# Order of the head's first operations, and rows of A gathered by GpSimd for half of the last level, in a graph layer on one core

## The chip, the cores and the metric

The kernel runs on one core of a Trainium2 chip. The metric is the device time of one execution in microseconds (us). The engines are called as the profile calls them: PE (TensorE; PEld is its loading of weights), DVE (VectorE), ACT (ScalarE), POOL (GpSimd) and SP (SyncE, which here only issues DMAs).

## The reference, cut to what matters

One layer of a graph network over 12500 nodes with 64 features and 212500 edges, sorted by their destination. `row` is the source of an edge, `col` its destination; sums go to the source.

```python
h = jnp.maximum(_layernorm(x, axis=-1), 0.0)
edge_in = jnp.concatenate([h[row], h[col], dist], axis=1)      # 64 + 64 + 1
e = jax.nn.silu(edge_in @ eW1 + eb1)                           # 128
e = jax.nn.silu(e @ eW2 + eb2)
agg = jax.ops.segment_sum(e, row, num_segments=h.shape[0])
node_in = jnp.concatenate([h, agg], axis=1)
out = x + jax.nn.silu(node_in @ nW1 + nb1) @ nW2 + nb2
```

## The kernel before

The first product splits into A = h @ eW1[:64] for the source, B = h @ eW1[64:128] for the destination, and a term of the edge weight. Nodes are dealt to 100 buckets of 125 (node = l * 100 + b). The tables `ta` (A) and `tb` (B) lie in DRAM with 256 floats for each node: a part rounded to fp32r and the remainder, each of 128.

**Sending.** Edges go in 208 blocks of 1024. For each block a window of `tb` is loaded (`load`), PE picks the rows (`qp`, line 531), ACT copies them to `qs` with the place l + 1 of the source in its bucket behind them (lines 543, 546), and POOL scatters 128 rows at a time to DRAM `q` by indirect DMAs (line 553), to places that VectorE has counted (`count`, lines 457 to 485). `q` then holds, bucket by bucket, the row Q of every edge without its A.

**Steps.** 14 levels take so many ranks of every bucket; a level goes over 25 batches of 4 buckets, a batch has n steps (1 or 2) of 512 edges, 450 steps in all. In the first and in the last level n is 1. `fetch` loads a batch's Q (`qt`, SP), `fetch_a` its A rows (`a`, SP, 512 KB, a ring of 3 buffers). A step is cut in pieces that `turn` puts in a fixed order (PE, DVE, ACT and SP run in the order written; POOL's queue is made by the framework):

- `s_one`: DVE compares the places with 1 to 125, which gives the one-hot `one` (line 719), three steps ahead.
- `s_turn`, `s_one_t`: PE turns it (`lr`, line 668), ACT copies it (`oneT`, line 673), two steps ahead.
- `s_pt`: PE transposes Q into `pt` (line 685) and adds A by products of A's two parts with `oneT` (line 692); ACT takes silu (line 701). One step ahead. It also asks for the next Q and A (`fetch` up to 4 batches ahead, `fetch_a` 3), and in the last level for the node's inputs (`nodes_in`: `xr`, to which POOL adds the bias at line 335, and `zo`).
- `s_bias`, `s_p2`: the second product and silu (lines 730, 736, 740).
- `s_seg`, `s_add`: PE sums by source (line 753), DVE adds to `aggT` (lines 762, 764).
- In the last level `nodes` follows each batch: PE's z product into the bank `misc` (line 348), ACT's silu (349), PE's o product (358), DVE's `os` (361) and its copy of the next `zo` into `misc` (363), and the store.

Four hooks in a step (`None` in `turn`) take in pieces of the sending, of `made_a`, of the feed (the `tb` rows) and of the node's tail.

**Level 0.** `made_a` makes A itself for each batch: it loads hT (`hrl`, line 642), multiplies (288), splits (292, 295), writes `ta` (647), computes the node part `zos` (651, 654) into a buffer of which there is one, and writes it to `own` (656).

**Head.** The first rows of x are normed (`norm`), multiplied (`first_rows`) and written to a small table, the first destinations (`destinations`) and sources (`sources`) are turned into places; the order of these operations is written out by hand, and so are the queues.

Of the kernel before, what the change touches and what calls it, by code (L numbers as in the profile page):

```python
# [28 lines left out]
F32 = mybir.dt.float32  # L29
# [3 lines left out]
I32 = mybir.dt.int32  # L33
# [6 lines left out]
P = 128  # L40
# [39 lines left out]
def tile_gnn(ctx: ExitStack, tc: tile.TileContext, x, src, dst, ew, eW1, eb1, eW2, eb2, nW1, nb1, nW2, nb2, out):  # L80
# [108 lines left out]
    def load_sources(h):  # L189

        at = h * BLK
        for p0, p1, n in ((0, 96, BLK), (96, NP - 1, BLK), (NP - 1, NP, min(BLK, LAST - at))):
            nc.sync.dma_start(srcR[p0:p1, at : at + n], vec(src, p0 * PAIR + at, p1 - p0, n))
# [81 lines left out]

    tb0 = dram.tile([P * NE, 2 * H], F32, name="tb0")
    tb00 = dram.tile([P * G, 2 * H], F32, name="tb00")
    ta_buckets, tb_buckets = (t.rearrange("(l b) f -> l b f", b=NB) for t in (ta, tb))

    def product(s, hr, ps, tag, to):  # L280
# [93 lines left out]
    with work:  # L374
# [21 lines left out]
        def load_rows(s):  # L396

            if s < nblocks and (s < 4 or stored):
                p, g = s // 2, s % 2
                if g == 0:  # L400
                    for a in range(2):
                        at = a * HB + WL
                        nc.sync.dma_start(extras[p % 2][at : at + 2], ews[:, p, :, a])
# [9 lines left out]
        def load(s):  # L413

            if s < nblocks:
                p, g = s // 2, s % 2
                win = wins[p % NW]
                table, end = (tb0, NE * P) if s < EARLY else (tb, NB * P)
                if s < 2 * FIRST_PAIRS:
                    table, end = tb00, G * P  # L420
                assert s < EARLY or len(done_b) == NB // G
                if g == 0:
                    of = identb[:, p % HB :: HB][:, :, None].to_broadcast([P, 2, HB])
                    nc.scalar.copy(sels[p % NW].rearrange("p (a m) -> p a m", a=2), of)
                    at = nc.sync.value_load(base_i[:, p : p + 1], min_val=0, max_val=end - SPAN)
                    for a in range(2):
                        rows = table[bass.ds(at, SPAN), :]
                        of = [[2 * H, WL], [4 * STEP * H, 2], [1, 2 * H]]
                        of = bass.AP(tensor=rows.tensor, offset=rows.offset + 2 * a * STEP * H, ap=of)
                        nc.sync.dma_start(win[a * HB : a * HB + WL, :, a].rearrange("p g k h -> p g (k h)"), of)  # L430
                blk[s] = [win[:, g], ld.tile([P, HALF], F32, name="pick")]
            load_rows(s + 1)
# [172 lines left out]
        def fetch(i):  # L605
            if i >= len(batches):
                return
            c, B, n = batches[i]
            assert not any(pending[: c + 1])
            at = B * G * ROWS + G * (ENDS[c] - n * P)  # L610
            qt = ld2.tile([P, G * most, W], F32, name="qt")
            ins = nc.sync.dma_start(
                qt[:, : G * n, :].rearrange("p j w -> p (j w)"),
                q[at : at + G * n * P, :].rearrange("(p j) w -> p (j w)", p=P),
            ).ins
            for later in range(c + 1, len(LEVELS)):
                tc.declare_no_dep(ins, group=f"rows{later}", reason="these ranks were full before")
            tc.add_manual_dep(ins, last_rows[LEVELS[c][1] - 1].name, AFTER)
            tc.add_to_no_dep_group("loads", ins)
            batch[c, B] = [qt, None, None]  # L620

        def fetch_a(i):

            if i >= len(batches):
                return
            c, B, n = batches[i]
            a = lda.tile([P, G, 2 * H], F32, name="a")
            if c == 0:
                making[B] = made_a(B, a)
                next(making[B])  # L630
            else:
                nc.sync.dma_start(a, ta_buckets[:, B * G : B * G + G])
            batch[c, B][1] = a
# [3 lines left out]
        def made_a(B, a):  # L637

            while B not in done_b:
                next(feed)  # L640
            hr = late.tile([P, G // 2, P], F32, name="hrl")
            nc.sync.dma_start(hr, hd[:, B * G // 2 : (B + 1) * G // 2, :])
            for _ in range(3):
                yield
            yield from product(0, hr, mm, "mm", a.rearrange("p g (k h) -> p g k h", k=2))
            yield
            nc.sync.dma_start(ta_buckets[:, B * G : B * G + G], a)
            zo = [mm.tile([P, G // 2, L], F32, name="zo", tag="mm") for _ in range(2)]
            for h in range(2):
                half = slice(h * D, (h + 1) * D)  # L650
                nc.tensor.matmul(zo[h], w1n[half, :], hr[half, :, :L], start=True, stop=True)
            zos = late1.tile([P, G * L], F32, name="zos")
            for h in range(2):
                nc.scalar.copy(zos.rearrange("p (i a l) -> p i a l", a=2, l=L)[:, :, h], zo[h])
            yield
            nc.sync.dma_start(own[:, B, :], zos)
            yield

        def of(k):
# [2 lines left out]
            return batch[c, B], [((g * G + t) % n * G + (g * G + t) // n, (g * G + t) // n) for t in range(G)]  # L662

        def s_turn(k):
            tops = st[k]["one"].rearrange("p g l -> p (g l)").bitcast(BF16)
            lr = mm.tile([L, G, P], F32, name="lr", tag="mm")
            for t in range(G):
                nc.tensor.matmul(lr[:, t, :], tops[:, 2 * t * L + 1 : 2 * (t + 1) * L : 2], identb, start=True, stop=True)  # L668
            st[k]["lr"] = lr

        def s_one_t(k):
            oneT = wk.tile([L, G, P], F32, name="oneT")
            nc.scalar.copy(halves(oneT), st[k].pop("lr"))  # L673
            st[k]["oneT"] = oneT

        def s_pt(k):

            (qt, a, _), tiles = of(k)
            c, B, _, _ = steps[k]
            for _ in making.pop(B, ()) if c == 0 else ():  # L680
                pass
            oneT = st[k].pop("oneT")
            pt = mm.tile([P, G, P], F32, name="pt", tag="mm")
            for t, (j, _) in enumerate(tiles):
                nc.tensor.matmul(  # L685
                    pt[:, t, :], qt[:, j, :H], ident, is_transpose=True, start=t == 0, stop=False, skip_group_check=True
                )
            for b, same in itertools.groupby(range(G), lambda t: tiles[t][1]):
                same = list(same)
                cols = slice(same[0], same[-1] + 1)  # L690
                for i in range(2):
                    nc.tensor.matmul(  # L692
                        pt[:, cols, :],
                        halves(a[:L, b, i * H : (i + 1) * H]),
                        halves(oneT[:, cols, :]),
                        start=False,
                        stop=i == 1,
                        skip_group_check=True,
                    )
            e1 = wk.tile([P, G, P], F32, name="e1")  # L700
            nc.scalar.activation(e1, pt, AF.Silu)  # L701
            st[k]["e1"] = e1
            c, B, n, g = steps[k]
            if c == len(LEVELS) - 1:
                node_in[B] = nodes_in(B, ndp[0])
            if g == n - 1:
                i = c * (NB // G) + B
                while len(fetched) <= i + NQ and (len(fetched) < final or i + 3 >= final):
                    fetched.append(0)
                    fetch(len(fetched) - 1)  # L710
                fetch_a(c * (NB // G) + B + NA)
# [247 lines left out]
        with listing:  # L959
# [5 lines left out]
            consts, zone_ = tables(), zones()  # L965
            next(rows_)
            next(consts)
            next(lists_)
            limits()
            next(rows_)  # L970
            next(firstw)
            next(lists_)
            nc.scalar.copy(halves(three2[:, 0, :]), three)
            nc.gpsimd.tensor_tensor(three2[:, 1, :], three, three2[:, 0, :], op=OP.subtract)
            last_rows_of(wins[0])
# [2 lines left out]
                last_rows_of(win)  # L978
            for xs in xss:
                nc.gpsimd.memset(xs, 0.0)  # L980
            next(rows_)
            next(src0)
            next(lists_)
            next(made[0])
            for part_ in (src0, made[0], firstw, made[0], made[0], lists_, src0, consts):
                next(part_)
            load_rows(0)
            load(0)
            load_sources(1)
            load(1)  # L990
            for part_ in (lists_, zone_):
                next(part_)
# [29 lines left out]
        aggT = aggp.tile([P, NB, L], F32, name="aggT")  # L1022
        late = work.enter_context(tc.tile_pool(name="late", bufs=3))
        late1 = work.enter_context(tc.tile_pool(name="late1", bufs=1))
        ld2 = work.enter_context(tc.tile_pool(name="ld2", bufs=NQ))
        lda = work.enter_context(tc.tile_pool(name="lda", bufs=NA))
        ones_ = work.enter_context(tc.tile_pool(name="ones", bufs=NO))
# [202 lines left out]
```

## Time and profile before

| | us |
|---|---|
| median of 3 runs | 3503.77 |
| lowest and highest | 3501.37, 3517.39 |
| the profiled execution's own time | 3483.84 |
| its span in the profile | 3482.0 |

In the views, a row of the timeline has start, duration, engine, line, operation, out<-in and the idle time of the engine ahead of it with what ended it. L719 is line 719; "q" behind an engine's name is its sequencer, which issues DMAs. A row of groups has the count, busy time and mean of one in ns. Times are of one profiled execution. "issue" is time in which an engine waited for nothing that the profile shows.

### The profile page before, as it was taken

How to read it: one execution, taken by the hardware profiler on the slowest of the kernel's cores; microseconds unless marked ns; L12 is line 12 of the kernel's file. 1: busy time of each engine (PE TensorE's matmuls, PEld its weight loads, DVE VectorE, ACT ScalarE, POOL GpSimd, SP SyncE). 2: the span in 40 equal slices, each digit the busy share in tenths (PEclk: the TensorE clock that was granted, in tenths of full speed). 3: DMA queues.
4: the chain of work that ended last, by engine and by line, in shares of the span. 5: the costliest groups of instructions: out<-in, count | busy, mean ns of one | idle time of the engine just before them, and what ended most of it. 6: DMA issues, size and time to landing. Idle time of an engine off the chain costs nothing. (4 is left out here: it accounts for less than half of the span.)

```text
span 3482.0 us, 47653 instructions
## 1 busy us (share of the span) xinstructions
PE 2344.1 (67%) x16730; PEld 2160.0 (62%) x16772; DVE 1842.7 (53%) x2884; ACT 1380.4 (40%) x3001; POOL 1641.7 (47%) x1724
## 2 busy tenths in 40 slices
PE   4445777735776567656765676767777767776799
PEld 3234666634665567556755666766676766766797
DVE  8775566554546445544454444455554554555443
ACT  3223444322444344334433444434443434443454
POOL 7665555465445544444445444444444544444401
PEclk7555778866887788778877888888888888888899
DMA  4344566654544345445553445455555655555586
GB/s 153 136 162 165 174 203 213 196 165 144 175 147 155 130 137 169 137 133 157 170 169 130 146 163 161 145 160 165 171 169 152 186 163 163 172 175 158 164 260 188
DMA packets 243744, 572.56 MB, mean 164 GB/s; under 512 B 47069, under 2 KB 106133, under 8 KB 243191
## 3 DMA queue, kind: packets, MB, share of 16 engines
q1 hardware_dynamic: 160308, 393.28, 36.6%
q0 software_dynamic: 53408, 122.68, 9.8%
q10 hardware_dynamic: 29782, 53.47, 4.8%
q8 instruction: 136, 2.23, 0.3%
q14 instruction: 110, 0.90, 0.1%
HBM read 349.93 MB, written 219.27 MB: 163 GB/s over the span
## 5 line engine op out<-in xcount | busy, mean ns | idle before, releaser
L553 POOL DMA_INDIRECT q<-qs,to x1661 | 1604.8, 966 | 1672.4 <-ACT qs L546 1174.1
L692 PE MATMUL pt<-oneT,a 125*128 125x128 f32 (+1 forms) x2800 | 491.9, 320 | 621.3 <-ACT oneT L673 518.8
L692 PEld LDWEIGHTS pt<-oneT,a 125*128 125x128 f32 x2800 | 415.3, 222 | 667.8 <-ACT oneT L673 552.5
L701 ACT ACTIVATE e<-pt 128x512 f32<-128x512 f32 x450 | 268.9, 598 | 1087.3 <-PE pt L692 374.4
L764 DVE TENSOR_TENSOR aggT<-aggT,seg 128x500 f32<-128x500 f32 x324 | 218.3, 674 | 876.0 <-remote 266.0
L736 PE MATMUL p<-w,e 128*128 128x128 f32 x3600 | 597.1, 319 | 0.0
L753 PE MATMUL seg<-one,e 128*128 128x125 f32 x3592 | 557.8, 303 | 51.1 <-DVE aggT L764 32.8
L736 PEld LDWEIGHTS p<-w,e 128*128 128x128 f32 x3600 | 548.1, 230 | 24.3 <-issue 22.4
L753 PEld LDWEIGHTS seg<-one,e 128*128 128x128 f32 x3592 | 498.1, 213 | 69.7 <-DVE aggT L764 37.9
L531 PE MATMUL qp<-win,pick 128*128 128x256 f32 x1664 | 379.4, 363 | 101.0 <-issue 49.2
L719 DVE TENSOR_TENSOR one<-misc,qt 128x500 f32<-128x500 f32 x425 | 286.0, 673 | 288.7 <-remote 75.4
L531 PEld LDWEIGHTS qp<-win,pick 128*128 128x128 f32 x1664 | 299.6, 248 | 184.1 <-issue 85.0
L543 ACT COPY qs<-qp 128x512 f32<-128x512 f32 x418 | 245.5, 588 | 406.4 <-issue 147.2
L740 ACT ACTIVATE e<-p 128x512 f32<-128x512 f32 x450 | 268.9, 598 | 278.8 <-remote 151.4
L465 DVE TENSOR_REDUCE each<-oh 128x100 bf16<-128x800 bf16 x208 | 318.3, 1530 | 7.2
L673 ACT CAST oneT<-lr 125x512 fp32r<-125x512 f32 x450 | 263.8, 586 | 101.8 <-remote 49.2
L685 PE MATMUL pt<-ident,qt 128*128 128x128 f32 x1800 | 284.8, 282 | 11.4 <-issue 5.0
L481 DVE TENSOR_TENSOR terms<-oh,misc 128x800 f32<-128x800 bf16 x208 | 203.6, 979 | 128.2 <-remote 95.4
L730 ACT COPY p<-b2f 128x512 f32<-128x512 f32 x450 | 267.1, 593 | 0.0
L685 PEld LDWEIGHTS pt<-ident,qt 128*128 128x128 f32 x1800 | 220.6, 147 | 28.5 <-issue 12.9
L483 DVE TENSOR_REDUCE rank<-terms 128x8 f32<-128x864 f32 x208 | 219.0, 1053 | 7.2
L668 PEld LDWEIGHTS <-one 128*125 128x125 bf16 x1800 | 197.5, 161 | 28.4 <-issue 27.0
(163 smaller groups left out, 1736.7 us busy)
## 6 DMA issues: line engine op xcount, KB each, us to landing
a<-ta SPq DMA_DIRECT2D x325, 512.0 KB
qt<-q SPq DMA_DIRECT2D x250, 288.0 KB
qt<-q SPq DMA_DIRECT2D x100, 576.0 KB
q<-zeros ACTq DMA_DIRECT2D x25, 1080.0 KB
q<-qs,to POOLq DMA_INDIRECT x1661
win<-tb SPq DMA_DIRECT2D x208, 120.0 KB
tb<-got SPq DMA_DIRECT2D x30, 512.0 KB
q<-zeros ACTq DMA_DIRECT2D x20, 720.0 KB
```

Source lines behind the costliest of these rows:

```text
L465: nc.vector.tensor_reduce(each, oh.rearrange("p t b -> p b t"), AX.X, OP.add)
L531: nc.tensor.matmul(qp[:, t % 2, :k], halves(pick[:, t * P : (t + 1) * P]), halves(win[:, :k, v]), start=v == 0, stop=v == 1,)
L553: ins = nc.gpsimd.indirect_dma_start(out=q[:], out_offset=bass.IndirectOffsetOnAxis(ap=to[:k, j : j + 1], axis=0), in_=qs[:k, t % 2, a, :] ...
L673: nc.scalar.copy(halves(oneT), st[k].pop("lr"))
L685: nc.tensor.matmul(pt[:, t, :], qt[:, j, :H], ident, is_transpose=True, start=t == 0, stop=False, skip_group_check=True)
L692: nc.tensor.matmul(pt[:, cols, :], halves(a[:L, b, i * H : (i + 1) * H]), halves(oneT[:, cols, :]), start=False, stop=i == 1, skip_group_c ...
L701: nc.scalar.activation(e1, pt, AF.Silu)
L719: nc.vector.tensor_tensor(one.rearrange("p (b j) l -> p b j l", j=n), (spots if c < len(LEVELS) - 1 else nodes1)[:, None, None, :].to_broa ...
L730: nc.scalar.copy(p2, b2f)
L736: nc.tensor.matmul(p2[:, t, :], e1[:, t, :], w2, start=False, stop=t == G - 1, skip_group_check=True)
L740: nc.scalar.activation(e2, p2, AF.Silu)
L753: nc.tensor.matmul(item[2][:, b, :], e2[:, t, :], one[:, t, :], start=j < G, stop=j >= G * (n - 1))
```

## The change

1. The order in the head. The norm of the first rows, the first sources and the first rows' transposes now stand ahead of the first destinations on ACT; the first weights' subtraction and store go behind the table's store; the second half of the sources is loaded on SP ahead of the first window (`load_sources(1)` before `load(0)`).
2. In level 0, `made_a` adds A's two parts on DVE into `a32`, in the one buffer that `zos` uses (now 512 floats instead of 500), and SP writes it to a third table `ta32` with 128 floats for each node, 256 KB a batch.
3. In the last level, the batches 0, 2, ..., 24 are picked up (`picked_up`). For these `fetch_a` lets POOL compute the row of each edge's source from the places in `qt` (three operations on 128x4) and gather the rows by four indirect DMAs of 128 rows of 512 bytes into the first half of A's buffer; `s_turn` does nothing; `s_one_t` adds the rows to `qt` on DVE; `s_pt` only transposes. `shift` holds b - 100 for each bucket.

```diff
+    ta32 = dram.tile([P * NB, H], F32, name="ta32")
...
+        def picked_up(c, B):
+            return c == len(LEVELS) - 1 and B % 2 == 0
...
         def fetch_a(i):
...
+            if picked_up(c, B):
+                qt = batch[c, B][0]
+                near = wk.tile([P, G], F32, name="near")
+                nc.gpsimd.tensor_scalar(near, qt[:, :G, H], 1.0, float(NB), op0=OP.max, op1=OP.mult)
+                row_of = wk.tile([P, G], I32, name="row_of")
+                nc.gpsimd.tensor_tensor(near, near, shift[:, B * G : B * G + G], op=OP.add)
+                nc.gpsimd.tensor_copy(row_of, near)
+                rows = lda.tile([P, G, 2 * H], F32, name="a")
+                batch[c, B][1] = rows
+                for t in range(G):
+                    nc.gpsimd.indirect_dma_start(
+                        out=rows[:, t, :H],
+                        out_offset=None,
+                        in_=ta32[:],
+                        in_offset=bass.IndirectOffsetOnAxis(ap=row_of[:, t : t + 1], axis=0),
+                    )
+                return
             a = lda.tile([P, G, 2 * H], F32, name="a")
...
-            zos = late1.tile([P, G * L], F32, name="zos")
+            zos = late1.tile([P, G * H], F32, name="zos", tag="zos")[:, : G * L]
...
             nc.sync.dma_start(own[:, B, :], zos)
             yield
+            a32 = late1.tile([P, G, H], F32, name="a32", tag="zos")
+            nc.vector.tensor_tensor(a32, a[:, :, :H], a[:, :, H:], op=OP.add)
+            nc.sync.dma_start(ta32.rearrange("(l b) f -> l b f", b=NB)[:, B * G : B * G + G, :], a32)
+            yield
...
         def s_turn(k):
+            if picked_up(*steps[k][:2]):
+                return
...
         def s_one_t(k):
+            if picked_up(*steps[k][:2]):
+                qt, rows, _ = batch[steps[k][:2]]
+                nc.vector.tensor_tensor(qt[:, :G, :H], qt[:, :G, :H], rows[:, :, :H], op=OP.add)
+                return
...
-            oneT = st[k].pop("oneT")
+            oneT = st[k].pop("oneT", None)
...
-            for b, same in itertools.groupby(range(G), lambda t: tiles[t][1]):
+            for b, same in itertools.groupby(range(G), lambda t: tiles[t][1]) if oneT is not None else ():
...
             next(rows_)
             next(consts)
-            next(lists_)
             limits()
             next(rows_)
+            next(rows_)
+            next(src0)
+            next(made[0])
+            next(lists_)
             next(firstw)
-            next(lists_)
...
-            next(rows_)
-            next(src0)
-            next(lists_)
             next(made[0])
-            for part_ in (src0, made[0], firstw, made[0], made[0], lists_, src0, consts):
+            for part_ in (src0, lists_, lists_, made[0], made[0], firstw, src0, lists_, consts):
                 next(part_)
             load_rows(0)
+            load_sources(1)
             load(0)
-            load_sources(1)
             load(1)
...
+        shift = aggp.tile([P, NB], F32, name="shift")
+        nc.vector.tensor_scalar(shift, nodes1[:, :NB], -float(NB + 1), None, op0=OP.add)
```

More of the change, by code (lines that the diff above doesn't have):

```diff
@@ L685, in s_pt @@
                 nc.tensor.matmul(
-                    pt[:, t, :], qt[:, j, :H], ident, is_transpose=True, start=t == 0, stop=False, skip_group_check=True
+                    pt[:, t, :],
+                    qt[:, j, :H],
+                    ident,
+                    is_transpose=True,
+                    start=t == 0,
+                    stop=oneT is None and t == G - 1,
+                    skip_group_check=True,
                 )
-            for b, same in itertools.groupby(range(G), lambda t: tiles[t][1]):
+            for b, same in itertools.groupby(range(G), lambda t: tiles[t][1]) if oneT is not None else ():
                 same = list(same)
```

## The prediction

> **What bounds the kernel now.** I read the page first, then the busy time by stage, then the chain that ended last, then the timelines of the three places that the change touches.
>
> ```profile
> span 3482.0 us, 47653 instructions
> PE 2344.1 (67%) x16730; PEld 2160.0 (62%) x16772; DVE 1842.7 (53%) x2884; ACT 1380.4 (40%) x3001; POOL 1641.7 (47%) x1724
> ```
>
> No engine is full over the whole span, so what a change is worth depends on its stage. The change touches three: the head (the first 30 us), level 0 (25 steps, about 311 to 551 us), and the last level (25 steps from about 3340 us on). The second view gives the busy time of each engine in two of them; the columns are PE, PEld, DVE, ACT, POOL, then granted clock, DMA share and GB/s.
>
> ```profile
> 311.00:551.00 240.00, 186.71 (x1154) 157.68 (x1152) 140.99 (x230) 101.58 (x255) 123.15 (x128) 0.76 0.57 190
> ```
> ```profile
> 3352.00:3463.00 111.00, 111.00 (x892) 99.39 (x891) 46.97 (x83) 61.23 (x108) 15.68 (x22) 1.00 0.77 238
> ```
>
> The last level is PE's alone: 111.00 of 111.00 us busy at the full granted clock, with POOL nearly idle. Level 0 is nobody's alone. The chain that ended last (start, duration, what) shows one step of the last level, and then a step that has no more tiles to prepare:
>
> ```profile
> 3457.94 0.96 PE o L358 x8
> 3458.90 0.24 PE lr L668 x4
> 3459.14 0.94 PE seg L753 x8
> 3460.09 0.44 PE pt L685 x4
> 3460.52 0.84 PE pt L692 x8
> 3461.36 0.89 PE misc L348 x2
> ...
> 3463.15 0.98 PE o L358 x8
> ...
> 3464.55 0.61 DVE misc L363
> 3465.16 0.65 DVE aggT L764
> ...
> 3465.85 1.10 PE misc L348 x2
> ```
>
> A step lasts from one o to the next, 3463.15 - 3457.94 = 5.21 us. Two of its pieces go in a picked-up batch: the turned one-hot (lr, 0.24) and the product with A (pt L692, 0.84), together 1.08 us. From o to the following z product (misc L348) an ordinary step takes 3461.36 - 3457.94 = 3.42 us. In the last steps lr and both pt are gone, and still it takes 3465.85 - 3463.15 = 2.70 us: there the chain is o, then VectorE's os, its copy into misc, its aggT, then z. So behind PE's queue lies a VectorE chain only 0.72 us shorter.
>
> **The last level, part by part.** Of 25 batches 13 are picked up. Batch j loses lr two iterations before its step and the A product one iteration before; both losses fall between one o and the z that follows it. PE alone would save 1.08 us, the VectorE chain lets through 0.72. I take 0.72 for each of the 11 pairs in the steady part: -7.9 us. The bounds: 13 x 1.08 = -14.0 if VectorE gave way, and nothing, or a loss, if the gathered rows come late. ScalarE also drops 13 copies of oneT, but at 61.23 of 111.00 us busy it is not late here.
>
> What it adds: for a picked-up batch POOL runs three small operations on 128x4, four indirect DMAs, and VectorE one addition of 128x512. The addition stands in VectorE's queue behind the one-hot of the next batch and ahead of os; whoever waits for the rows holds os, misc, aggT and with them z. So the deadline is the next os, not the step that needs the rows. The rows for the chain:
>
> ```profile
> 3406.91 0.42 DVE L361 TENSOR_TENSOR os<-o,xr 125x256 f32<-125x256 f32 x1 [2.82 <-issue]
> ...
> 3408.24 0.79 SPq L132 DMA_DIRECT2D xr<-in_x_dram  x2
> ...
> 3408.64 0.67 DVE L719 TENSOR_TENSOR one<-nodes,qt 128x500 f32<-128x500 f32 x1
> ...
> 3412.15 0.73 POOL L335 TENSOR_TENSOR xr<-xr,nb2b 125x256 f32<-125x256 f32 x1 [4.17 <-DMA xr<-in_x_dram]
> ```
> ```profile
> L553 POOL DMA_INDIRECT q<-qs,to x1661 | 1604.8, 966 | 1672.4 <-ACT qs L546 1174.1
> ```
> ```profile
> L132 SPq DMA_DIRECT2D xr<-in_x_dram x50: 323/392/1145, 3338.4 to 3460.7; - x50
> L335 POOL TENSOR_TENSOR xr<-xr,nb2b x25: 726/729/738, 3343.2 to 3462.7; 125x256 f32<-125x256 f32 x25
> ```
>
> POOL is in order, and its addition for xr stands ahead of the gathers: from os to that addition's start are 3412.15 - 3406.91 = 5.24 us, most of it the landing of xr. Then 0.73 for the addition; three small operations, which no row shows at this size: between nothing and 0.73 each (the larger addition), taken at 0.3, 0.9 in all; four gathers at 0.966 plus the gap between two DMAs, 0.30 (the first POOL row of the next fences), 5.06; the landing; and 0.67 for VectorE's addition, by the one-hot, which also reads two SBUF operands. No row shows a gather landing. The last xr was issued at 3460.7 and used at 3462.7, 2.0 us; in the crowded part it is 3412.15 - 3408.24 = 3.9. POOL's DMAs go through a queue of their own in the page, not behind SP's A load of 512 KB, so I take 2.0. Sum: 5.24 + 0.73 + 0.9 + 5.06 + 2.0 + 0.67 = 14.6 us. There are three steps to the os in question: one of 5.21 and a pair of 2 x 5.21 - 0.72 = 9.70, together 14.91. It fits, with 0.3 us to spare. At the entry of the level the steps are shorter and the first pick-ups wait for Q's load as well; I charge 3 us for the first two, an estimate: about one late landing of 2.0 and half of a second. Last level: -7.9 + 3 = -5 us; bounds -14 and +18 (below).
>
> A rule speaks against this part. In this case's head one indirect DMA took more than twice its usual time while VectorE ran an operation with two SBUF operands:
>
> ```profile
> 37.66 2.29 DVE L923 TENSOR_TENSOR ewR<-ewR,ewH 104x2048 f32<-104x2048 f32 x1
> ```
> ```profile
> 36.83 0.96 POOL L553 DMA_INDIRECT q<-qs,to  x1 [0.30 <-issue]
> 38.51 2.28 POOL L553 DMA_INDIRECT q<-qs,to  x1 [0.72 <-issue]
> ```
>
> The Trainium skill (SBUF — State Buffer, "SBUF: two separate sides") says that VectorE with two SBUF inputs and a GpSimd operation that reads SBUF hold one shared port pair by an exclusive lock. By that rule one gather of the four could be held for an addition of 0.67, and the chain would be 15.3. Over the whole run the mean of 1661 is 966 ns with VectorE busy half of the time, so I add nothing to the forecast; the late chain is a rival.
>
> **The table of float32 rows, in level 0.** Each of 25 batches adds a VectorE addition of 128x512 (0.67, as above), one more DMA issue on SP and 256 KB written. 6.5 MB more in a stage at 0.57 DMA share delays nothing by itself. But a32 takes the one buffer of zos: VectorE's addition waits until own has landed, behind it in VectorE's queue stand the subtraction for the next A and the counting; SP waits for the addition before it issues the write, with window and Q loads behind; and ScalarE's next zos waits until the write has landed, with all activations behind.
>
> ```profile
> 430.19 0.32 SPq L656 DMA_DIRECT2D own<-zos  x1
> ...
> 436.12 0.65 ACT L654 COPY zos<-zo 128x250 f32<-128x250 f32 x2
> ```
> ```profile
> L654 ACT COPY zos<-zo x50: 362/369/390, 311.4 to 551.3; 128x250 f32<-128x250 f32 x50
> ```
>
> The price: from own's issue to the next zos it now takes a landing, 0.67, an issue of 0.32, and a landing. A landing here lies between the 2.0 and the 3.9 of xr; at 3.1 the sum is 7.2. On the average batches come (551.3 - 311.4) / 24 = 10.0 us apart, which covers it; the close ones, such as 436.12 - 430.19 = 5.9, don't, and wait 1.3. If half of 24 wait so, ScalarE stands 16 us longer. It is busy 101.58 of 240 us, so I count half on the path: +8 us. The additions themselves (25 x 0.67 = 17) go into VectorE's idle 99 us; without that cover they cost those 17. Bounds: 0 and +37 (rival below).
>
> **The head.** The order of ScalarE's and SP's queues changes; nothing is added but one shift table (one small VectorE operation).
>
> ```profile
> 8.32 0.19 ACT L875 CAST firstf<-dstR 128x1 f32<-128x1 int32 x1 [2.28 <-DMA dstR<-in_dst_dram]
> ...
> 24.85 1.04 ACT L896 CAST sf<-srcR 104x1024 f32<-104x1024 int32 x1 [6.08 <-DMA srcR<-in_src_dram]
> 24.92 0.17 DVE L485 TENSOR_SCALAR to<-rank 128x8 int32<-128x8 f32 x1
> ...
> 27.02 1.28 POOL L553 DMA_INDIRECT q<-qs,to  x1 [7.05 <-ACT qs L546]
> ```
>
> The square root of the first rows stood behind the destinations' wait of 2.28; it now goes ahead. The second half of the sources held ScalarE for 6.08 us, and the first copies to qs stood behind it; its load now is issued ahead of the first window load on SP, which pays one issue time but waited for its table anyway. What is late next for the first scatter are its places, ready at 24.92 + 0.17 = 25.1 instead of the 27.02 at which POOL started: 1.9 us, and up to 2.3 more as the first rows come earlier. I take -3; bounds 0 (later stages swallow it) and -4.
>
> **Sum.** -3 + 8 - 5 = 0 against the profiled execution's 3483.84 us. The median of the runs shown is 3503.77, 19.9 us above it, which no row explains; I carry the difference over and forecast 3503.8 us. From the terms that are likely together its own range is some 3493 to 3516.
>
> **The rivals.** 0.5% of this kernel, 17.5 us, is about what a measurement of it can tell from no change.
>
> A, slower: the gather chain sets the pair. With the small operations at 0.73 each and landings of 3.1, the chain is 5.24 + 0.73 + 2.2 + 5.06 + 3.1 + 0.67 = 17.0 us; a pair then takes 17.0 - 5.21 = 11.8 against 10.42 before, 11 x 1.4 = +15 instead of -8, with the entry +18. Result 3527. It decides as soon as the chain passes 14.9, and costs more than before past 15.6. For it: only 0.3 us to spare, and 3.9 us seen for xr. Against: POOL's own ring.
>
> B, slower: the shared buffer in level 0. With landings of 4.0 us the sum is 9.0, half of the batches (gap 5.9) wait 3.1 on ScalarE, and none of it is hidden: 24 x 0.5 x 3.1 = 37 instead of 8. Result 3503.8 + 29 = 3533. For it: ScalarE and VectorE feed each other there at every step; against: each is idle for over a third of the stage.
>
> C, faster: VectorE gives way, so that each pick-up saves the full 1.08 us (-14), level 0 hides everything, and the head brings its -4: -18, result 3486, just past the bound. For it: PE busy all of the time in the last level; against: the 2.70 us row.
>
> D, no gain in the last level: the VectorE chain or the rows leave nothing of the 0.72. -3 + 8 = +5, result 3509, within the bound.
>
> **How the numbers follow.** Forecast 0.52, D 0.11 (both within 0.5%), A 0.12 and B 0.13 (slower), C 0.12 (faster). Faster 0.12, same 0.63, slower 0.25. The range takes in C's time and most of A: 3485 to 3529; it leaves out B and part of the tails of C and A, about 0.2.
>
> **What would show it.** In the profile after: the first scatter at 23 to 25 us instead of 27.02, and ScalarE no longer idle for the second srcR; in level 0 a wait of zos for a DMA of a32, some 10 to 20 us in total, and 25 additions of 0.67; in the last level pairs of steps of about 9.7 us where 10.42 stood, with z ended last by VectorE's aggT, four gathers of about 1 us each, and the VectorE addition not idle ahead for longer than the slack. I am wrong on the last level if VectorE idles ahead of that addition for a gather in most pairs, on level 0 if its 25 steps take over 20 us longer or not longer at all, on the head if POOL's start doesn't move.

## The result and the profile after

| | before | after |
|---|---|---|
| median, us | 3501.85 | 3536.84 |
| lowest and highest | 3475.79, 3520.56 | 3517.73, 3557.39 |
| the profiled execution's own time | 3483.84 | 3517.73 |

The change is slower: the ratio of after to before is 1.0091, 95% interval [1.0067, 1.0116]. The forecast was no change, 3503.8 us in 3485 to 3529; the result lies 8 us above the range. The two profiled executions are 33.9 us apart, nearly the 35.0 us of the medians, so they can be compared.

The head of the page of after, its span and the busy time of the engines:

```profile
span 3516.0 us, 47560 instructions
PE 2350.5 (67%) x16574; PEld 2161.0 (61%) x16616; DVE 1863.5 (53%) x2923; ACT 1379.2 (39%) x2988; POOL 1710.2 (49%) x1815
```

PE does 156 matmuls fewer, as the 13 picked-up steps should bring, and VectorE and POOL are busy 21 and 69 us longer. None of that tells where 34 us went, so the first question is in which stage they are. The silu of each step (ACT, e<-pt) marks its time in the timeline; the time from the first silu of a level to that of the next, worked out from the 450 rows (for the last level to its last silu):

```
us         to first silu   level 0   levels 1-11   level 12   level 13
before             321.7     247.9        2647.2      124.7      119.9
after              317.4     274.0        2651.7      127.3      125.0
difference          -4.3     +26.1          +4.5       +2.6       +5.1
```

So the head gives 4 us, level 0 takes 26, and the last two levels, which were to bring 5, take 8. Levels 1 to 11, in which nothing is changed, are 4.5 longer; single profiles scatter there by more than that (below).

**The head.** Rows of the timeline of after, ACT and POOL:

```profile
6.81 0.21 ACT L829 ACTIVATE var<-var 128x4 f32<-128x4 f32 x1 [0.79 <-DVE var L828]
...
21.46 1.05 ACT L933 CAST sf<-srcR 104x1024 f32<-104x1024 int32 x1 [5.50 <-DMA srcR<-in_src_dram]
...
24.82 2.14 POOL L554 DMA_INDIRECT q<-qs,to  x1 [3.23 <-ACT qs L547]
```

The first scatter starts at 24.82 instead of 27.02, but ScalarE still stands 5.50 us for the second srcR (6.08 before), only 3.4 us earlier.

**Level 0.** The stage table (its columns as in the prediction), the longest waits of that stretch, and the answers about two writes, own's (L677) and a32's (L681, which the profile calls ta<-a): how often each was issued, and who waited for it how long and how many times.

```profile
307.00:590.00 283.00, 198.55 (x1280) 166.72 (x1278) 170.58 (x277) 114.58 (x276) 140.23 (x144) 0.79 0.60 204
```
```profile
POOL q L554 <- ACT qs L547: 100.4, 20, 14.6
DVE a L680 <- DMA own<-zos: 47.9, 15, 7.7
```
```profile
L677 SPq DMA_DIRECT2D own<-zos x25: 319/320/1427, 307.8 to 565.2; - x25
...
who waited for it (us, times):
  DVE a L680: 55.2, 16
  ACT zos L675: 5.3, 2
```
```profile
L681 SPq DMA_DIRECT2D ta<-a x25: 319/320/355, 317.4 to 569.5; - x25
...
who waited for it (us, times):
  DVE a L680: 4.2, 2
  ACT zos L675: 2.7, 2
```

The wait that I priced, ScalarE's zos behind the write of a32, is 2.7 us in two places. (Its 5.3 us behind own are no news: in before they were 5.5, in two places too.) The wait that I named and did not price is VectorE's: 15 of 25 additions stand ahead of its whole queue until own has landed, 47.9 us in all. (The answer about own's write counts one more, of 7.3 us, which the list of waits puts down to issue.) One of them, in the timeline:

```profile
355.78 0.17 DVE L486 TENSOR_SCALAR to<-rank 128x8 int32<-128x8 f32 x1
...
358.87 0.60 ACT L738 ACTIVATE e<-pt 128x512 f32<-128x512 f32 x1 [5.17 <-remote]
...
360.76 0.77 ACT L675 COPY zos<-zo 128x250 f32<-128x250 f32 x2 [1.29 <-PE zo L672]
...
361.55 0.32 SPq L677 DMA_DIRECT2D own<-zos  x1
...
363.63 0.69 DVE L680 TENSOR_TENSOR a<-a 128x512 f32<-128x512 f32 x1 [7.67 <-DMA own<-zos]
364.24 0.98 DVE L458 TENSOR_TENSOR oh<-misc,bkt 128x800 bf16<-128x800 f32 x1
```

VectorE was free at 355.95. The zos that fills the buffer was not even copied then: PE's product and ScalarE's copies, which come after a silu that stood 5.17 us, last until 361.53; then SP issues own, and the last 2.1 us are the DMA. Behind the addition waits the next block's counting (L458). In half of the 16 waits own is already on its way; over all of them, worked out from the timeline, 37 of the 55 us lie behind SP's issue of own, which takes 1.8 to 5.3 us to land (median 2.0).

**The last level.** The waits for the gathers, and the timeline of POOL and VectorE from one addition to the next:

```profile
DVE qt L701 <- DMA a<-ta,row_of: 17.7, 12, 5.0
```
```profile
3430.32 0.69 DVE L701 TENSOR_TENSOR qt<-qt,a 128x512 f32<-128x512 f32 x1 [1.18 <-DMA a<-ta,row_of]
...
3431.76 1.04 POOL L641 DMA_INDIRECT a<-ta,row_of  x1 [2.00 <-DVE qt L701]
...
3435.62 0.95 POOL L641 DMA_INDIRECT a<-ta,row_of  x1 [0.31 <-issue]
...
3438.59 0.20 POOL L636 TENSOR_TENSOR near<-near,shift 128x4 f32<-128x4 f32 x1
3438.86 0.19 POOL L637 CAST row_of<-near 128x4 int32<-128x4 f32 x1
...
3440.17 0.69 DVE L701 TENSOR_TENSOR qt<-qt,a 128x512 f32<-128x512 f32 x1 [0.35 <-DMA a<-ta,row_of]
...
3441.61 1.04 POOL L641 DMA_INDIRECT a<-ta,row_of  x1 [2.56 <-DVE qt L701]
```

POOL has the next rows' numbers by 3439.05 (L637), and still the next gather starts only 0.75 us after VectorE's addition (3440.86 to 3441.61). So the pick-ups gather, it seems, into one and the same buffer of A's ring of three, and each waits for the one before it to be used up. (The profile leaves out the buffers' numbers; the waits say it, and rows2 below tests it.) That closes a loop: addition 0.69, 0.75 to the gather, four gathers 4.8 (3431.76 to 3436.57), their landing 3.6 here (to 3440.17; 3.6 to 4.4 over eight pick-ups of the steady part, mean 4.1; at the ends of the level also less, down to 2.2). 0.69 + 0.75 + 4.8 + 4.1 = 10.3 us, close to the 10.42 that a pair took before and the 10.54 that it takes in after.

### The profile page after: what moved, and what is told of

Read it like the earlier page. It is cut to its first block, busy times and chain, and to the rows that moved or that the text cites. A ratio compares the mean times of both kernels' runs of the same rounds, so it can differ in the third digit from the quotient of the medians.

```text
span 3516.0 us, 47560 instructions
## 1 busy us (share of the span) xinstructions
PE 2350.5 (67%) x16574; PEld 2161.0 (61%) x16616; DVE 1863.5 (53%) x2923; ACT 1379.2 (39%) x2988; POOL 1710.2 (49%) x1815
## 4 chain that ended last, share of the span: by engine, by line
PE 48%; another core or an unknown queue 18%; ACT 10%; issue 8%; DVE 5%; DMA 2%; POOL 1%; SPq 1%; ACTq 0%; DVEq 0%; POOLq 0%
PE p L773 12%; PE seg L790 10%; PE pt L729 10%; PE qp L532 5%; PE pt L716 4%; PE lr L695 3%; ACT oneT L704 2%; ACT e L777 2%; ACT e L738 2%; ACT p L767 2%; PE bc L411 1%; ACT qs L544 1%; DVE aggT L801 1%; DVE each L466 1%
## 5 line engine op out<-in xcount | busy, mean ns | idle before, releaser
L729 PE MATMUL pt<-oneT,a 125*128 125x128 f32 (+1 forms) x2696 | 479.6, 322 | 630.0 <-ACT oneT L704 512.3
L729 PEld LDWEIGHTS pt<-oneT,a 125*128 125x128 f32 x2696 | 403.6, 224 | 674.3 <-ACT oneT L704 543.0
L773 PE MATMUL p<-w,e 128*128 128x128 f32 x3600 | 605.2, 322 | 0.0
L773 PEld LDWEIGHTS p<-w,e 128*128 128x128 f32 x3600 | 556.1, 233 | 24.2 <-issue 21.4
L544 ACT COPY qs<-qp 128x512 f32<-128x512 f32 x418 | 245.3, 587 | 377.7 <-issue 116.3
L704 ACT CAST oneT<-lr 125x512 fp32r<-125x512 f32 x437 | 256.4, 587 | 106.6 <-remote 58.2
```

The lines of the kernel that those rows point to most:

```text
L729: nc.tensor.matmul(pt[:, cols, :], halves(a[:L, b, i * H : (i + 1) * H]), halves(oneT[:, cols, :]), start=False, stop=i == 1, skip_group_c ...
L773: nc.tensor.matmul(p2[:, t, :], e1[:, t, :], w2, start=False, stop=t == G - 1, skip_group_check=True)
```

## Experiments

The theory after these readings: two shared buffers cost what the change loses, own's in level 0 (+26 us by VectorE's wait) and A's in the last level (no gain in the steady part, some loss at the entry). The rivals: the added work itself (VectorE's 25 additions, 6.5 MB written), the new head, or the entry of the last level. The first four kernels ran where the kernel before takes 2302.47 us, the others where it takes 3505 to 3510 like the runs above; a ratio is always to the kernel before on the same chip. What was expected as a time of level 0 or as a ratio was worked out from the slower chip's times for the first four, and from the faster one's for the others.

**head**: the new order of the head alone.

```diff
-            return c == len(LEVELS) - 1 and B % 2 == 0
+            return False
...
-            yield
-            a32 = late1.tile([P, G, H], F32, name="a32", tag="zos")
-            nc.vector.tensor_tensor(a32, a[:, :, :H], a[:, :, H:], op=OP.add)
-            nc.sync.dma_start(ta32.rearrange("(l b) f -> l b f", b=NB)[:, B * G : B * G + G, :], a32)
```

> The change's new order of the head alone: no table of float32 rows, no pick-ups. Head theory: POOL's first scatter starts at 24 to 25 us instead of 27.0, the first silu of level 0 comes about 4 us earlier, level 0 lasts about 248 us as before, and the total is 0 to 5 us below before (ratio 0.999 to 1.000). Rival: the earlier start itself puts level 0's steps out of step with the feed and makes level 0 some 20 us longer; then the ratio is 1.005 or more.

Measured: 2301.68 us, ratio 1.0005 [0.9989, 1.0022]. The head is worth nothing that can be seen.

**table**: the new head and the table in level 0, which nobody reads (only `return False` above).

> The new head and the float32 table made in level 0, but no batch picked up: the table is written and not used. If level 0 carries the loss (theory), level 0 lasts 270 to 278 us instead of 248, VectorE waits 40 to 60 us in total for own's landing ahead of its addition, and the ratio is 1.005 to 1.009. If the last level carries it (rival), the ratio is within 0.002 of the head alone.

Measured: 2339.94 us, ratio 1.0164 [1.0143, 1.0186]. Level 0 takes 231.9 us where head has 189.4: +42.5, as much as the whole loss (the two profiles' spans are 43.2 us apart), and more than expected. Its waits in that stretch:

```profile
DVE a L680 <- DMA own<-zos: 63.4, 17, 7.8
ACT e L738 <- PE pt L729: 63.4, 25, 10.4
POOL q L554 <- ACT qs L547: 46.5, 14, 9.4
...
PEld pt L716 <- DVE pick L447: 17.0, 2, 8.5
```

VectorE's wait is again first, and the sending starves behind it: PE waits for VectorE's picks, POOL for the copies to qs. Of the 63.4 us 54 lie behind SP's issue of own, which takes 2.0 to 7.2 us to land here (median 3.4). In the row below VectorE is free at 296.80; SP had issued own at 295.77, by its timeline:

```profile
300.84 0.69 DVE L680 TENSOR_TENSOR a<-a 128x512 f32<-128x512 f32 x1 [4.04 <-DMA own<-zos]
```

**own32**: the whole change, but a32 in the ring of qs instead of own's buffer.

```diff
-            a32 = late1.tile([P, G, H], F32, name="a32", tag="zos")
+            a32 = qsp.tile([P, 2, 2, W], F32, name="qs").rearrange("p a b w -> p (a b w)")[:, : G * H]
+            a32 = a32.rearrange("p (g f) -> p g f", g=G)
```

> The whole change, but a32 takes a buffer of the ring of eight that the sent rows use, and not the one of zos. Theory (VectorE's addition stands waiting for own's landing and holds what is behind it): the wait is gone, level 0 lasts 248 to 256 us, the total falls by 18 to 26 us against the change, ratio to before 1.001 to 1.004. Rival (the additional work itself: 25 additions, 25 issues, 6.5 MB of writes): level 0 stays at 268 us or more and the ratio above 1.007.

Measured: 2317.55 us, ratio 1.0073 [1.005, 1.0095]. Level 0 takes 198.7, +9.3 instead of +42.5. The same addition (now L681; three of the 25 stand ahead of this window) and what VectorE waited for ahead of it:

```profile
L681 DVE TENSOR_TENSOR qs<-a x22: 670/685/722, 267.7 to 439.1; 128x512 f32<-128x512 f32 x22
its engine sat idle before it (us, times) until:
  DMA q<-qs,to: 3.8, 2
```

The same work and the same bytes, another buffer, and 33 of the 42 us are gone: that part is shown. The ratio misses the 1.001 to 1.004 of the theory all the same, and by itself would fit the rival's (above 1.007): level 0 keeps 9.3, and the last two levels, with their gathers still in one buffer, add 5.4. The last level is not helped (121.6 us against head's 119.9).

**rows2**: the whole change, but every second pick-up gathers into a buffer of its own, so that no two in a row share one.

```diff
-                rows = lda.tile([P, G, 2 * H], F32, name="a")
+                rows = late1.tile([P, G, H], F32, name="rows", tag="zos") if B // 2 % 2 else lda.tile([P, G, 2 * H], F32, name="a")
```

> The whole change, but every second pick-up gathers into the buffer of zos, so that two pick-ups in a row never share a buffer. Theory (a gather waits for the addition before it, because both use one buffer; that loop of about 10.6 us sets the pair of steps): POOL's wait for VectorE's addition ahead of the first gather is gone, the pair falls from 10.5 to 9.7 to 10.2 us, the last level gets 5 to 9 us shorter, ratio about 1.007. Rival (the landing of the rows and POOL's own queue set the pair): the pair stays above 10.4 and VectorE's addition goes on waiting for the gathers, over 15 us in total.

Measured: 2338.27 us, ratio 1.0161 [1.0138, 1.0184] (level 0 has own's shared buffer, as in table: 229.9). The last level takes 114.9 us, 5.0 less than head. A pair of steps, from ScalarE's silus in the timeline, and what VectorE waited for ahead of its 13 additions of the level:

```profile
2291.89 0.60 ACT L738 ACTIVATE e<-pt 128x512 f32<-128x512 f32 x1 [1.64 <-PE pt L729]
2296.01 0.60 ACT L738 ACTIVATE e<-pt 128x512 f32<-128x512 f32 x1 [1.55 <-PE pt L716]
2301.80 0.60 ACT L738 ACTIVATE e<-pt 128x512 f32<-128x512 f32 x1 [1.64 <-PE pt L729]
```
```profile
  DMA a<-ta,row_of: 5.8, 3
  issue: 3.1, 1
  DMA rows<-ta,row_of: 2.6, 3
```

2301.80 - 2291.89 = 9.91 us, where own32 has 10.26 and head 10.41; in own32 VectorE waits for the gathers 29.4 us at all 13 additions, here 8.4 at 6, and POOL no longer stands for VectorE ahead of a gather. The last level of each kernel, by its silus:

```
us         first 7 steps   8 pairs, each   last step
before              31.4           10.42        5.21
after               36.6           10.54        4.13
head                31.4           10.41        5.20
own32               35.4           10.26        4.12
rows2               31.6            9.90        4.12
```

On the faster chip (head, own32, rows2) the shared buffer takes 0.36 of the 0.51 us that a pair can gain and makes the first seven steps 3.8 us longer. It does not hold every pair: in own32 five of the eight take 9.90 to 9.91 as in rows2, and one 11.46. What stays with two buffers is level 12: 98.5 us in rows2 and 99.0 in own32, against 95.3 in head and 95.6 in table, +3.2 at the entry.

**after2, both, two, twolate**: the change as it is; own32 and rows2 together; no table at all, rows of 1024 bytes gathered from the two parts in `ta` with two additions; and the same only from batch 4 on. The edit of two:

```diff
-                        out=rows[:, t, :H],
+                        out=rows[:, t, :],
...
-                        in_=ta32[:],
+                        in_=ta[:],
...
-                nc.vector.tensor_tensor(qt[:, :G, :H], qt[:, :G, :H], rows[:, :, :H], op=OP.add)
+                for i in range(2):
+                    nc.vector.tensor_tensor(qt[:, :G, :H], qt[:, :G, :H], rows[:, :, i * H : (i + 1) * H], op=OP.add)
```

> The change as it is, beside before on the chip of these experiments, so that its parts and the whole can be set side by side. If the parts add up (head 0, table +38, last level about +5 of 2302 us), the ratio is 1.016 to 1.021, level 0 lasts 229 to 233 us, the last level 121 to 122. If the parts interact, the whole is off this sum by over 8 us.

> The whole change with both cures: a32 in the ring of the sent rows, and the pick-ups taking turns in two buffers. If the two cures are independent: level 0 about 199 us, last level about 115, ratio 1.003 to 1.006, that is still slower than before by what the table costs. Rival (the table costs nothing once its buffer is free, and the 9 us left in level 0 are of another kind): ratio 0.998 to 1.001.

> No table at all: the pick-ups gather rows of 1024 bytes from ta, both parts of A, and VectorE adds twice. Level 0 about 189 us as with the head alone. For the last level: if the loop over one buffer set the pair, and the rows now rotate over the ring (the gathers of this version wait for PE instead of the addition before), the pair is 9.8 to 10.2 us and the ratio 0.998 to 1.001. Rival (twice the bytes and a second addition of 0.69 us on VectorE's chain): the pair is 10.4 us or more and the ratio 1.001 to 1.004.

> As the version without a table, but picked up only from batch 4 on (11 batches of 25, not 13). If the first two pick-ups cost some 3 us at the entry of the last level, because their Q has just been asked for, the level before lasts 95 us as with the head alone, and the total falls by another 2 to 4 us: ratio 0.996 to 0.999, below before. Rival (the entry costs nothing): no difference to the version without a table beyond 1 us.

| | median, us | ratio | level 0 | level 13 |
|---|---|---|---|---|
| after2 | 3550.13 | 1.0091 [1.0058, 1.0124] | 270.5 | 125.0 |
| both | 3518.79 | 1.0021 [0.9989, 1.0053] | 245.3 | 118.5 |
| two | 3536.82 | 1.0077 [1.0051, 1.0102] | 248.7 | 125.5 |
| twolate | 3518.35 | 1.0033 [1.0006, 1.006] | 255.4 | 122.2 |

Where the kernel before takes 3510, too, the two other buffers give back 31 of the 40 us (3550.13 to 3518.79); both lies between what its theory and its rival expected, and its interval reaches into both. after2 ran on the slower chip, so it does not tell whether the parts add up. The kernel two missed its expectation, and its rival's: without a table level 0 is as before, but the last two levels take 14 us more than before. There POOL does not stand for VectorE ahead of a gather either, and still a pair takes 10.83 us, with twice the bytes and a second addition. Its answer about the additions:

```profile
L698 DVE TENSOR_TENSOR qt<-qt,a x24: 686/692/693, 3383.0 to 3498.6; 128x512 f32<-128x512 f32 x24
...
  DMA a<-ta,row_of: 18.2, 9
```

VectorE still waits for gathers, up to 5.7 us, and does 0.69 more per pick-up. Levels 1 to 11, in which nothing is changed, were 2684.0 us there against 2650.0 in twolate's profile; how much of the 26 us in the median is the last level and how much that stretch stays open. twolate was expected below before and is not (1.0033).

**half, halflate, addonly, writeonly**: attempts to part the 9.3 us that level 0 keeps, and at a version that pays. half is both with a table for the 13 picked-up batches only; halflate the same with pick-ups from batch 4 on; addonly has VectorE's addition in the ring of qs, no write and no pick-ups; writeonly has the write from A's first half, no addition and no pick-ups.

```diff
+            if picked_up(len(LEVELS) - 1, B):
                 a32 = ...
-            return c == len(LEVELS) - 1 and B % 2 == 0
+            return c == len(LEVELS) - 1 and B % 2 == 0 and B >= 4
```

> The change with a32 in the ring of qs, rows of every second pick-up in late1's buffer, and the float32 table made and written only for the 13 batches that are picked up (52 buckets in place of 100). Theory (level 0 pays for each batch that adds and writes; the pick-ups save what they save without a shared buffer): level 0 gets +9.3 x 13/25 = +5 us, level 12 (entry) +3, level 13 -5: +3 in all, ratio 1.001 where the kernel before takes 2302 us and 1.001 where it takes 3500. Rival (level 0's +9 is the price of one disturbed order, whatever the number of batches): +9 +3 -5 = +7, ratio 1.003.

> As half, with batches 0 and 2 of the last level left as they were before: 11 pick-ups from batch 4 on, and a table for 44 buckets. Theory (the 3 us of level 12 are the first two pick-ups, which wait for Q's load, gathers and landing ahead of the level's first steps): level 12 goes back to within 0.5 us of the kernel without pick-ups, level 13 keeps -4, level 0 pays 11/25 of 9.3 = 4.1: 0 in all, ratio 1.000. Rival (any first pick-up costs its landing, wherever it stands): the same 3 us turn up in level 13, which then gains only 1 to 2 us: ratio 1.002.

> The head's new order, and in level 0 VectorE's addition of A's two parts into a buffer of the ring of qs; no table is written and nothing is picked up (the addition's result is not used). It parts the +9.3 us that level 0 keeps when own's buffer is not shared. Theory (VectorE feeds each step there, so 25 additions of 0.69 us = 17 us lie on the path for about half, and a buffer of qs is held a little longer): level 0 +6 to +9, ratio 1.003 to 1.004. Rival (the write of 6.5 MB is what costs): level 0 +0 to +2, ratio 1.000 to 1.001.

> The head's new order, and in level 0 SP writes 256 KB a batch into the float32 table straight from the first half of A's buffer, with no addition by VectorE; nothing is picked up (the table then holds only A's rounded part and is not used). Theory (the addition on VectorE costs, the bytes don't): level 0 +0 to +3, ratio 1.000 to 1.001. Rival (6.5 MB more at a DMA share of 0.8, and one more issue on SP ahead of its window and Q loads): level 0 +6 to +9, ratio 1.003 to 1.004.

| | median, us | ratio | level 0 | level 13 |
|---|---|---|---|---|
| half | 3517.06 | 1.0026 [1.0003, 1.005] | 250.8 | 123.9 |
| halflate | 3509.25 | 1.0006 [0.998, 1.0031] | 252.5 | 118.6 |
| addonly | 3510.69 | 1.0014 [0.9988, 1.004] | 255.3 | 119.9 |
| writeonly | 3509.32 | 1.0006 [0.9982, 1.0029] | 253.2 | 119.9 |

These do not tell the cases apart: the intervals hold both theory and rival (in writeonly the rival's 1.003, the cost of the bytes, lies just outside), and level 0 of single profiles here (245 to 255 us in every kernel without own's shared buffer, 247.9 before) moves as much as the 9.3 us in question. half's last level misses the expected gain: its pairs are 10.55 us with separate buffers, where both has 10.08 and rows2 9.90. POOL waits for Q's load ahead of the row numbers in all three (14.1, 16.9 and 14.2 us over about 100 us), so that does not explain it. On the slower chips, then, the gain of separate buffers is not steady (10.08 in both, 10.20 in halflate, 10.55 in half, against 10.54 and 10.62 with a shared one); the clean evidence is the faster chip's. No version beats the kernel before.

## Why the prediction was wrong

**Level 0: the term that failed.** The sum had +8, measured +26.1, and +42.5 on the faster chip, where the profiles repeat to some 2 us (231.9 in table, 229.9 in rows2, which share the buffer alike). The step that failed is in the change part: it said that VectorE's addition waits until own has landed, with its queue behind it, and then priced only the other end of the buffer, ScalarE's next zos behind a32's write. That wait is 2.7 us (7.0 in table); VectorE's, to which the sum gave nothing, is 47.9 (63.4). The cost of the addition was put at 0.67 in idle time, and an idle share says nothing of an in-order engine that stands still: what counts is when the addition's turn comes, and in some two thirds of the batches it comes before own has landed. The bound of +37 for zos, rival B, came to 3533 us, near the result, with the right buffer and the wrong engine: that nearness is luck. On the slower chip a part of the 26 may be something else: ScalarE's silus stood 35.9 us there for what the profile calls remote, 22.2 in before; on the faster chip no such wait stands in the profiles. With another buffer the term is +9.3, about the +8 of the sum, by another way: no such wait, so perhaps the 17 us of additions half hidden (VectorE is busy 157.69 of 198.00 us there); that is argued, not shown.

```profile
253.00:451.00 198.00, 164.19 (x1232) 142.81 (x1231) 157.69 (x259) 107.04 (x266) 142.10 (x147) 0.89 0.82 276
```

**Last level: right mechanism, missed loop.** With a buffer for each of two pick-ups a pair takes 9.90; the sum had 9.70. That VectorE's chain lets through less than PE's 1.08 us was right: 0.51 of 10.41 arrived, 0.72 was forecast, and z waits for VectorE's aggT, as said (in rows2, 6.4 us in 10 places between 2215 and 2310 us). PE, busy 100.00 of 100 us in head, is busy 95.19 in rows2. In the change as it is the pair stays at 10.54. Two steps failed. The landing was taken at 2.0 by the last xr, with the 3.9 of the crowded part kept as an end: 4.1 was measured. And the chain of 14.6 us was laid from os through POOL's order to the addition; that the gather must also wait for the addition before it, since the pick-ups use one buffer of the ring, stands in no row of before. That loop of 10.3 us needs both, the shared buffer and the late landing: with 2.0 it would be 8.2 and decide nothing; and half, with separate buffers and no gain, stays unexplained. Rival A (pairs that the gather chain sets) has the right place; the price is not its 11.8.

**Entry.** 3 us were charged to two late pick-ups. Level 12 takes 3.2 more with separate buffers, so the size was right; with the shared one the first seven steps of the level pay 3.8 more.

**Head.** The first scatter moved by 2.2 us into the forecast 23 to 25, and the first silu by 4.3. As a gain of the whole nothing is seen of it (head, 1.0005 [0.9989, 1.0022], which still leaves room for 2.5 us); the bound 0, that later stages swallow it, is the nearest. ScalarE's wait for srcR did not go, against what I had written.

**The port.** The small operations were put at 0.3 between 0 and 0.73. In after's timeline above one took 0.20. In rows2 the same one ran beside VectorE's addition:

```profile
2262.09 0.69 DVE L701 TENSOR_TENSOR qt<-qt,rows 128x512 f32<-128x512 f32 x1
```
```profile
2262.34 0.49 POOL L636 TENSOR_TENSOR near<-near,shift 128x4 f32<-128x4 f32 x1
```

It ended at 2262.83, just after the addition's 2262.78. By the rule of the Trainium skill that was weighed (SBUF — State Buffer, "SBUF: two separate sides") POOL is locked out for the rest of such an operation, and this row agrees. It cost tenths of a microsecond, so leaving it out of the sum was right.

**Sum.** Head -4.3, level 0 +26.1, levels 1 to 11 +4.5, level 12 +2.6, level 13 +5.1: +34.0 where 0 was forecast. 18 us of the miss are level 0, 13 the last two levels.

## What to carry to other kernels

When an operation takes a buffer that something else fills or reads, price the wait on the engine that will stand in line, from when its turn comes to when the buffer comes free: the other engine's turn and the landing of the DMA, which was the larger part here (37 of 55 us in after, 54 of 63 in table). An idle share covers work, not waits. Where a transfer fills a buffer whose reader releases the next transfer, write the loop down (use, issue, transfer, landing) and compare it with the period it must hold; one more buffer is the cheapest test.

## What was not expected of the hardware

- Four gathers of 128 rows of 512 bytes reach VectorE 3.6 to 4.4 us after POOL's last gather row has ended (the steady part of after); xr's last load took 2.0 from issue to use.
- The kernel before took 2302.47 us on one chip and 3505 to 3510 on two others, and each held its own time through all runs. On the slower ones the engines stand for something that the profile can only call remote. The group of the first silus on the page of after, and of head, which ran on the faster chip (behind the second bar the idle time ahead of the group, and what ended most of it):

```profile
L738 ACT ACTIVATE e<-pt 128x512 f32<-128x512 f32 x450 | 269.3, 598 | 1116.8 <-remote 365.1
```
```profile
L734 ACT ACTIVATE e<-pt 128x512 f32<-128x512 f32 x450 | 268.7, 597 | 502.0 <-PE pt L725 497.2
```

  After the sending the last level takes 119.9 us on both (before and head). In the traces of before and after every wait called remote (298 and 300 of them, 1188 and 1190 us summed over the engines) ends with a count of the semaphore that PE's matmuls raise, in the median 3.4 us after the end given for PE's last matmul: so these waits point at PE, not at something outside the core (the ends of matmuls are modelled, so this is not certain). Why PE is late there was not found. A cost that shows in the steps of the faster chip (+9.3 in level 0, where profiles repeat to some 2 us) drowns on the slower ones.
